# A two-layer graph attention kernel on one core: the order of the encoder's last additions, the place of the decoder's first weights on VectorE, and the queue that stores kept tiles

## Chip, core and metric

The kernel runs on one core of a Trainium2 chip. The metric is the device time of one execution in microseconds (us); the median of several runs counts. Engines are named as in the profile: PE (TensorE), ACT (ScalarE), DVE (VectorE), POOL (GpSimd), SP (SyncE). PEld is PE's loading of weights.

## What is computed

Layer 0, for N = 4096 nodes, 512 features and H = 4 heads of D = 128 (both masks of the layer are the same adjacency matrix, so its two attentions are one):

```python
Xw  = einsum('hnd,hde->hne', Xh, W)              # Xh: relu(layernorm(x)) by heads
sig = sigmoid(f1[:, :, None] + f2[:, None, :])   # f1, f2: Xw times V
att = softmax(where(adj != 0, adj * sig, -inf))  # per head, 4096 x 4096
Xn  = batchnorm(concat_heads(att @ Xw))
emb = batchnorm(elu(Xn @ Wm.T + bm) + Xn)        # encoder's MLP
Y   = elu(concat_heads((att @ Yh) @ W.T))        # Yh: emb by heads; the same att again
out = batchnorm(elu(Y @ Wd.T + bd) + Y)          # decoder's MLP
x   = x + out
```

Layer 1 is a graph attention layer with leaky-relu logits over the same adjacency matrix, with a residual. The change touches layer 0 alone.

## The kernel before

**Blocks and tiles.** `attention` (L221) runs three times: for the encoder (L598), the decoder (L702) and layer 1 (L932). Each run goes over 8 blocks: 4 heads, and for each the two halves `tb` of 2048 target nodes. A block goes over NJ = 32 source groups `j` of 128 nodes. For each `j` a tile `e` of 128 x 2048 fp32 unnormalized weights is made and multiplied on PE with the head's values (L371) into four PSUM banks, one for each 512 targets. In the encoder and decoder the weights come from `tanh_weights` (L448): a tanh on ACT (L450), an exp on ACT (L451) and a multiplication by the mask on DVE (L452).

**Masks.** The adjacency matrix comes as fp32. At the start POOL issues eight DMAs (L481) that cast it to uint8 into DRAM (`masks`). For each tile SP loads 128 x 2048 bytes of it (`load_mask`, L210, 256 KB) into one of five buffers `a`; the load waits until the multiplication five tiles earlier has been done.

**Buffers of weights.** The encoder has eight `e` buffers: two in the pool `keep` (EP = 2), which also the decoder uses, and six of its own. A tile's buffer is used again eight tiles later, when PE, the sums and a store, if there is one, have done with it.

**Denominators.** The sum of the weights over `j` is needed in the encoder. A schedule (ENC and others, L62 to L64) says for each `j` which way is taken: an accumulating DMA of POOL (L386, `moved`), a product with ones on PE (L262, `by_ones`), or else an addition on DVE into `acc` (L394). In the encoder's last block the tiles 30 and 31 go by ones, 26 to 29 by DVE. At the end of a block the sums themselves are multiplied by ones (L405, L407). In the last block the product of tile 31 is left until behind them (`late`, L376 and L423); then come the reciprocal (L435), its spreading on PE (L440), scaling and statistics. The encoder's MLP (`mlp_block`, L605) starts on PE with products of the first three heads (L613).

**Kept tiles.** The decoder needs the same weights again. The encoder (`kept="write"`) stores every fifth tile of a block (j = 4, 9, 14, 19, 24, 29; KEEP = 5) to DRAM in `ekeep`, 1 MB each, 48 in all. The store is issued by ACT three tiles later (L358), the block's last one at tile EVICT = 2 of the next block (through `at`, L292) or, in the last block, at its end (L410). The decoder (`kept="read"`) loads these tiles by SP (L343) instead of making them.

**The decoder's first weights.** Tiles 0 and 1 of the decoder use the two buffers of `keep`, so they can be made before the encoder's pools are released; tile 0 is made in four quarters. `pinned` (L213) makes instructions stand behind given ones in the order of issue.

**The order of the work** on each engine is fixed when the program is built: a scheduler places each instruction on its engine's queue, within the bounds that `issue_after` and `pinned` set; on the chip each queue then runs in that order. DMAs issued by SP, ACT and POOL appear in the profile as the queues q1, q10 and q0.

Of the kernel before, what the change touches and what calls it, by code (L numbers as in the profile page):

```python
# [42 lines left out]
NJ = N // P  # L43
# [27 lines left out]
KEEP = 5  # L71

EP = 2

EVICT = 2
# [10 lines left out]
def kernel(ctx, tc, x, xT, adjT, w0, w0T, v0, wencT, wdecT, vecs, w1, w1T, a1, outT):  # L86
    nc = tc.nc
# [131 lines left out]


    def attention(what, keep, pools, weights, values, row_of, out, finish, ebufs, modes=None, invert=None,  # L221
                  kept=None, sums=None, sums2=None, extras={}, row0=None, masks0=(), in_parts0=1):

# [64 lines left out]
        def at(j, f, *args):  # L290

            later.setdefault(j, []).append(lambda: f(*args))  # L292
# [28 lines left out]
        for n, (h, tb) in enumerate(blocks):  # L321
            last = n == len(blocks) - 1
            moved, by_ones, *ends_later = modes(n) if modes is not None else ((), ())
            den = bank1() if invert is not None else None
            begun = False
            into = sums2[0 if n else 1] if moved else None

            po, ahead, late = [bank() for _ in range(SB - 1)], [], []
            adds, held, stores, next_row = [], [], [], None
            for j in range(NJ):  # L330

                with pinned(products_of):
                    for f in later.pop(j, []):
                        f()
                with pinned([a_load, *products_of, last_main] if j else []):
                    if (n, j) in extras:
                        extras[n, j](a_load)
                    if not last and j == NJ - 10:
                        next_row = next_row_of(*blocks[n + 1])
                e = weight_tile()  # L340
                store = j % KEEP == KEEP - 1 and kept is not None
                if store and kept == "read":
                    a_load = nc.sync.dma_start(e, ekeep[h][tb][j // KEEP])  # L343
                else:
                    if masks0:
                        a, a_load = masks0.pop(0)
                    else:
                        a = mask_tile(keep)
                        a_load = load_mask(a, tb, j)

                    with pinned(products_of[:1] if kept == "read" and n == 0 and j < 8 else []):
                        products_of = weights(e, rowb, a, j, h, SB if NJ * n + j < in_parts0 else 1)
                    if store:
                        stores.append((j // KEEP, e))

                    if j % KEEP == KEEP - 3 and stores:
                        k, t = stores.pop()
                        nc.scalar.dma_start(ekeep[h][tb][k], t)  # L358

                def products():  # L360
                    nonlocal last_main, last_ones

                    with tc.issue_after(last_ones.ins) if last_ones is not None else nullcontext():

                        if j == EVICT:
                            po.append(bank())
                            for k, t in ahead:
                                nc.tensor.matmul(po[-1], block(values[h], k), t[:, (SB - 1) * IB:SB * IB],  # L368
                                                 start=(k == 0), stop=False)
                        for s, b in enumerate(po):  # L370
                            last_main = nc.tensor.matmul(b, block(values[h], j), e[:, s * IB:(s + 1) * IB],  # L371
                                                         start=(j == 0), stop=(j == NJ - 1))
                    last_ones = None


                if last and invert is not None and j >= NJ - (1 if kept is not None else 2):  # L376
                    late.append((j, e))
                else:
                    products()
                if j < EVICT:  # L380
                    ahead.append((j, e))
                if invert is not None:
                    if j in moved:

                        for into_half, e_half in in_parts(2, into, e):
                            nc.gpsimd.dma_start(into_half, e_half, **({"accum_op": ALU.add} if j > moved[0] else {}))  # L386
                    elif j in by_ones:
                        held.append(e)
                    else:
                        adds.append(e)  # L390
                        if len(adds) == 2:
                            nc.vector.tensor_add(acc, *adds)
                        elif len(adds) > 2:
                            nc.vector.tensor_add(acc, acc, e)  # L394

                    if held and j + 1 not in by_ones:
                        with tc.issue_after(last_main.ins):
                            for t in held:
                                add_to_den(den, t, not begun)
                                begun = True  # L400
                        held = []
                    if j == NJ - 1:
                        with tc.issue_after(last_ones.ins) if last_ones is not None else nullcontext():
                            if moved and not ends_later:
                                add_to_den(den, into, not begun)  # L405
                                begun = True
                            add_to_den(den, acc, not begun, not ends_later)  # L407
            for k, t in stores:
                if last:
                    nc.scalar.dma_start(ekeep[h][tb][k], t)  # L410
                else:
                    at(EVICT, nc.scalar.dma_start, ekeep[h][tb][k], t)
            if not last:

                at(EVICT, ending, h, tb, po, den if invert is not None else None,
                   4 if kept == "write" and n == 0 else 0)
                if ends_later:
                    at(1, add_to_den, den, into, False, True)
                rowb = next_row
                continue  # L420
            for s, b in enumerate(po):
                for k, t in late:
                    nc.tensor.matmul(b, block(values[h], k), t[:, s * IB:(s + 1) * IB], start=(k == 0),  # L423
                                     stop=(k == NJ - 1))
            outs = [out(spool, h, tb, s, po[s]) for s in range(SB)]
            if invert is None:
                for s, o in enumerate(outs):
                    rb = spread(h, tb, s)
                    for f in finish:
                        f(spool, h, tb, s, o, rb, True)  # L430
                continue

            inv = spool.tile([P, IB], FP, name="dsb", tag="rb", bufs=3)
            nc.vector.tensor_scalar(inv, den, invert[0], None, invert[1])
            nc.vector.reciprocal(inv, inv)  # L435
            if kept is not None:
                nc.gpsimd.dma_start(rinvs[h][tb].rearrange("o (s i) -> (o s) i", i=IB), inv[0:P:32, :])
            for s, o in enumerate(outs):
                rb = bank()
                nc.tensor.matmul(rb, ident[:, 32 * s:32 * s + 1].to_broadcast([P, P]), inv, start=True, stop=True)  # L440
                for f in finish:
                    f(spool, h, tb, s, o, rb, True)
# [14 lines left out]
    with tc.tile_pool(name="keep", bufs=1) as keep:  # L457
# [147 lines left out]
        def mlp_block(work, w, src, dst, gamma, beta, scale, between, early=None):  # L605
# [11 lines left out]
            for o in range(C):  # L617
# [7 lines left out]
                for ib in range(NIB):  # L625
# [13 lines left out]
                        nc.vector.tensor_add(d, nodes(src[o], ib), ex)  # L639
                    else:  # L640
                        nc.vector.scalar_tensor_tensor(d, nodes(src[o], ib), scale[:, o:o + 1], ex, ALU.mult, ALU.add)
                    nc.vector.bn_stats(stats[:, o, ib, :], d)
                    between(o, ib)
                bn_coefs(stats, gamma, beta, a_mlp, b_mlp, o, o + 1)
            return last_product

        with tc.tile_pool(name="m_small", bufs=1) as small, tc.tile_pool(name="m_work", bufs=3) as work:
# [4 lines left out]
                nc.vector.tensor_add(bias, bias_of(bank1(), C - 1, C)[:, 0:C], bias)  # L652
                scale_weights(C - 1)

            mlp_block(work, w, xc, yc, "enc_mlp_bn_gamma", "enc_mlp_bn_beta", a_att, lambda o, ib: None, last_head)


            for h in range(H):
# [41 lines left out]
        nc.sync.dma_start(w, wdecT.rearrange("(c p) o -> p c o", p=P))  # L700
        with tc.tile_pool(name="dec", bufs=1) as spool:
            attention("dec", keep, spool, tanh_weights, xc, lambda h, tb: (rows[tb], h), out_dec, (scaled, elu), 4,  # L702
                      kept="read", extras={(1, 6): sums_of_weights, (1, 16): bias_of_decoder})


    v1 = xd
# [2 lines left out]
    with tc.tile_pool(name="l_small", bufs=1) as small, tc.tile_pool(name="l_work", bufs=2) as work:  # L709
# [22 lines left out]
                nc.sync.dma_start(outT[o * P:(o + 1) * P, :], x1[o])  # L732
            return added

        def between(o, ib):

            if o in (1, 2):
                residual(o - 1, ib)
            elif o == C - 1 and ib >= NIB // 2:
                residual(o - 1, ib - NIB // 2)  # L740
# [237 lines left out]
```

## Time and profile before

| What | Value |
|---|---|
| Runs shown | 3267.72, 3262.49, 3267.79 us; median 3267.72 |
| Profiled execution | 3260.23 us, of which the span of the core is 3258.4 us |
| PE, DVE, ACT, POOL busy | 98%, 82%, 80%, 15% of the span |
| Encoder's attention | 65 to 1043 us |
| Encoder's MLP | 1055 to 1197 us |
| Decoder's attention | from 1197 us |
| Encoder's ACT in blocks 3 to 6 | 118.7 to 118.8 us each, with 118.6 to 118.7 busy |
| DMA packets | 578.48 MB; q0 36.0%, q1 27.1%, q10 4.8% of 16 engines' span |
| Stores of kept tiles | 48 of 1024 KB, median 7.6 us from issue to landing |
| Loads of masks | 720 of 256 KB, median 4.1 us from issue to landing |

How it is read: times in a timeline are us from the span's start. A group of instructions shows line, engine and operation, then the written tile, an arrow and the read tiles. In brackets stands how long the engine was idle just before, and who ended that. "x2" says that two like instructions were merged. A landing is the end of a DMA, as its semaphore tells it. Busy time of PE is no measure of its peak, since matmuls are pipelined and their ends are modelled; each 128 x 512 fp32 product appears as two records.

### The profile page before, as it was taken

Reading aid. Unit: us, or ns where it says so; the run is one execution under the profiler, and the core shown is the slowest. Engines: PE = TensorE matmul, PEld = TensorE weight load, DVE = VectorE, ACT = ScalarE, POOL = GpSimd, SP = SyncE. Lnnn points to the kernel's source line nnn. Section 1 sums busy time; section 2 is a strip of 40 time slices with the busy share of each in tenths; the row PEclk is TensorE's granted clock in tenths of the full one; section 3 lists DMA queues with packets and bytes.
Section 4 is the critical chain, followed back from the end, with each engine's and each line's share of the span. In section 5 each row is a group of like instructions: output and inputs, shape, how many; then the busy total and the mean of one; then the engine's idle time right before and its main releaser. Section 6 shows DMA issues by size and latency. Waiting matters only on the chain.

```text
span 3258.4 us, 26085 instructions
## 1 busy us (share of the span) xinstructions
PE 3197.5 (98%) x8723; PEld 1484.0 (46%) x8723; DVE 2665.4 (82%) x1933; ACT 2601.8 (80%) x1908; POOL 477.6 (15%) x622
## 2 busy tenths in 40 slices
PE   7999999999999999999999999999999999999999
PEld 6334434444443464444444444448644444444443
DVE  6999999999999675556655565585599999999998
ACT  7999999999997459899999999566765666666664
POOL 2001221211211000000000000025412222122221
PEclk9999999999999999999999999999999999999999
DMA  9997988988986014434443443231488999889995
GB/s 208 196 195 226 259 227 230 266 224 226 268 232 177 4 64 130 147 127 129 153 142 125 139 153 122 78 121 56 129 207 216 218 229 243 214 210 238 218 214 143
DMA packets 211150, 578.48 MB, mean 178 GB/s; under 512 B 25068, under 2 KB 28172, under 8 KB 195016
## 3 DMA queue, kind: packets, MB, share of 16 engines
q0 software_dynamic: 67968, 222.51, 36.0%
q1 hardware_dynamic: 126432, 293.72, 27.1%
q10 hardware_dynamic: 16616, 60.60, 4.8%
q8 instruction: 68, 1.11, 0.1%
q14 instruction: 66, 0.54, 0.0%
HBM read 377.10 MB, written 84.29 MB: 142 GB/s over the span
## 4 chain that ended last, share of the span: by engine, by line
PE 68%; ACT 12%; DVE 9%; issue 7%; DMA 3%; POOL 0%; ACTq 0%; DVEq 0%; POOLq 0%
PE ps L371 52%; ACT e L450 7%; PE ps L613 7%; DVE e L452 5%; ACT e L451 4%; PE ps L809 3%; DMA a<-mask 2%; DVE acc L394 2%; PE den L262 1%; DVE e L904 1%; DVE R L394 1%; PE ps L670 1%; DMA acc<-e 1%; PE ps L368 1%; PE ps L537 1%
## 5 line engine op out<-in xcount | busy, mean ns | idle before, releaser
L371 PE MATMUL ps<-e,R 128*128 128x512 f32 x6024 | 2614.1, 594 | 37.5 <-DVE e L452 35.2
L371 PEld LDWEIGHTS ps<-e,R 128*128 128x128 f32 x6024 | 1140.1, 190 | 1504.8 <-issue 1396.6
L452 DVE TENSOR_TENSOR e<-e,a 128x2048 f32<-128x2048 f32 (+1 forms) x470 | 1051.7, 2259 | 383.7 <-ACT e L451 369.4
L450 ACT ACTIVATE e<-rowb,score 128x2048 f32<-128x2048 f32 (+1 forms) x470 | 912.4, 1968 | 85.9 <-PE ps L371 43.9
L451 ACT ACTIVATE e<-e 128x2048 f32<-128x2048 f32 (+1 forms) x470 | 870.6, 1879 | 6.1
L903 ACT ACTIVATE e<-rowb,nq,jcol 128x2048 f32<-128x2048 f32 x224 | 461.4, 2090 | 273.7 <-DMA w<-e 133.9
L904 DVE SCALAR_TENSOR_TENSOR e<-e,jcol,a 128x2048 f32<-128x2048 f32 (+1 forms) x265 | 591.8, 2267 | 7.3 <-ACT e L903 7.3
L394 DVE TENSOR_TENSOR acc<-acc,e 128x2048 f32<-128x2048 f32 x130 | 297.1, 2286 | 2.1
L394 DVE TENSOR_TENSOR R<-R,e 128x2048 f32<-128x2048 f32 x123 | 280.5, 2281 | 0.0
L386 POOL DMA_DIRECT2D w<-e x178 | 150.3, 847 | 613.4 <-DMA w<-e 356.1
L613 PE MATMUL ps<-R,w 128*128 128x512 f32 x512 | 220.3, 592 | 0.6 <-DVE w L571 0.6
L386 POOL DMA_DIRECT2D acc<-e x144 | 120.4, 881 | 542.9 <-DMA acc<-e 196.8
L287 POOL DMA_DIRECT2D rb<-rinvs x60 | 34.5, 580 | 1059.2 <-DVE R L561 865.9
L613 PEld LDWEIGHTS ps<-R,w 128*128 128x128 f32 x512 | 97.2, 190 | 122.7 <-issue 117.7
L634 ACT ACTIVATE ex<-ps,bias 128x512 f32<-128x512 f32 x64 | 44.0, 687 | 98.8 <-PE ps L613 79.0
L809 PE MATMUL ps<-w1x,hT 128*128 128x260 f32 x512 | 115.5, 384 | 1.4 <-ACT hT L787 1.4
L809 PEld LDWEIGHTS ps<-w1x,hT 128*128 128x128 f32 x512 | 96.5, 190 | 19.9 <-issue 3.3
L903 ACT ACTIVATE e<-w,nq,jcol 128x2048 f32<-128x2048 f32 (+1 forms) x41 | 67.4, 1711 | 24.5 <-DMA R<-e 24.4
L636 DVE SCALAR_TENSOR_TENSOR ex<-ex,re 128x512 f32<-128x512 f32 x64 | 45.0, 702 | 36.4 <-ACT re L635 36.2
L846 POOL TENSOR_TENSOR vacc<-vacc,R 128x128 f32<-128x128 f32 x120 | 65.8, 576 | 45.3 <-ACT R L839 45.0
L839 ACT ACTIVATE R<-ps,rstd 128x128 f32<-128x128 f32 x128 | 38.5, 371 | 29.3 <-PE ps L809 25.6
L262 PE MATMUL den<-e,ones 128*32 128x512 f32 x424 | 51.1, 598 | 0.0
(172 smaller groups left out, 1246.2 us busy)
## 6 DMA issues: line engine op xcount, KB each, us to landing
a<-mask SPq DMA_DIRECT2D x720, 256.0 KB, 4.1
w<-e POOLq DMA_DIRECT2D x178, 512.0 KB, 6.8
acc<-e POOLq DMA_DIRECT2D x144, 512.0 KB, 6.7
ekeep<-e ACTq DMA_DIRECT2D x48, 1024.0 KB, 7.6
e<-ekeep SPq DMA_DIRECT2D x48, 1024.0 KB, 4.9
mask<-in_adjT POOLq DMA_DIRECT2D x8, 2048.0 KB, 99.4
rowb<-rows SPq DMA_DIRECT2D x16, 1024.0 KB, 7.7
rb<-rinvs POOLq DMA_DIRECT2D x60, 256.0 KB, 4.2
```

The costliest lines, as they stand in the source:

```text
L262: last_ones = nc.tensor.matmul(den[s * 32:(s + 1) * 32, :], ones[:, 0:32], t[:, s * IB:(s + 1) * IB], start=start, stop=stop)
L371: last_main = nc.tensor.matmul(b, block(values[h], j), e[:, s * IB:(s + 1) * IB], start=(j == 0), stop=(j == NJ - 1))
L386: nc.gpsimd.dma_start(into_half, e_half, **({"accum_op": ALU.add} if j > moved[0] else {}))
L394: nc.vector.tensor_add(acc, acc, e)
L450: nc.scalar.activation(e, rowb, AF.Tanh, bias=column(score[:, 1], j, h), scale=0.5)
L451: last_act = nc.scalar.activation(e, e, AF.Exp, scale=0.5)
L452: last_dve = nc.vector.tensor_mul(e, e, a)
L613: last = nc.tensor.matmul(z, w[:, fb, o * P:(o + 1) * P], nodes(src[fb], ib), start=(fb == 0), stop=(fb == C - 1))
L809: m = nc.tensor.matmul(banks[k][:, 0:2 * DX], hT[:, fb, c * P:(c + 1) * P], w1x[:, fb, 2 * k:2 * k + 2, :].rearrange("p h x -> p (h x)"), ...
L846: nc.gpsimd.tensor_add(vacc[:, h, :], vacc[:, h, :], block(v1[h], j))
L903: last_act = nc.scalar.activation(e, rowb, AF.Relu, bias=column(nq, j, h), scale=column(jcol, j, h))
L904: last_dve = nc.vector.scalar_tensor_tensor(e, e, column(jcol2, j, h), a, ALU.add, ALU.mult)
```

## The change

It has three parts. In the encoder's last block, additions on DVE of tiles from j = 26 on are collected and issued after the multiplication of tile 31; the first of them may be placed where its operands and the queue allow. The decoder's first two tiles are pinned behind the statistics of the MLP's output block 1, column step 0 (a DVE instruction, L642). The stores of kept tiles are issued by SP instead of ACT, and in the order of the program when the next kept tile is made, five tiles later, instead of three.

```diff
     def attention(what, keep, pools, weights, values, row_of, out, finish, ebufs, modes=None, invert=None,
-                  kept=None, sums=None, sums2=None, extras={}, row0=None, masks0=(), in_parts0=1):
+                  kept=None, sums=None, sums2=None, extras={}, row0=None, masks0=(), in_parts0=1, behind=()):
...
-                    with pinned(products_of[:1] if kept == "read" and n == 0 and j < 8 else []):
+                    with pinned([*(products_of[:1] if kept == "read" and n == 0 and j < 8 else ()),
+                                 *(behind if n == 0 and j < EP else ())]):
                         products_of = weights(e, rowb, a, j, h, SB if NJ * n + j < in_parts0 else 1)
                     if store:
+                        if stores:
+                            k, t = stores.pop()
+                            nc.sync.dma_start(ekeep[h][tb][k], t)
                         stores.append((j // KEEP, e))
-
-                    if j % KEEP == KEEP - 3 and stores:
-                        k, t = stores.pop()
-                        nc.scalar.dma_start(ekeep[h][tb][k], t)
...
                         adds.append(e)
-                        if len(adds) == 2:
+                        if last and kept is not None and j >= NJ - 6:
+                            at_end.append(e)
+                        elif len(adds) == 2:
                             nc.vector.tensor_add(acc, *adds)
                         elif len(adds) > 2:
                             nc.vector.tensor_add(acc, acc, e)
+
+                    if j == NJ - 1:
+                        for t in at_end:
+                            nc.vector.tensor_add(acc, acc, t)
...
             for k, t in stores:
                 if last:
-                    nc.scalar.dma_start(ekeep[h][tb][k], t)
+                    nc.sync.dma_start(ekeep[h][tb][k], t)
                 else:
-                    at(EVICT, nc.scalar.dma_start, ekeep[h][tb][k], t)
+                    at(EVICT, nc.sync.dma_start, ekeep[h][tb][k], t)
...
-                    nc.vector.bn_stats(stats[:, o, ib, :], d)
-                    between(o, ib)
+                    made = nc.vector.bn_stats(stats[:, o, ib, :], d)
+                    between(o, ib, made)
...
+            behind_it = []
+            mlp_block(work, w, xc, yc, "enc_mlp_bn_gamma", "enc_mlp_bn_beta", a_att,
+                      lambda o, ib, made: behind_it.append(made) if (o, ib) == (1, 0) else None, last_head)
...
             attention("dec", keep, spool, tanh_weights, xc, lambda h, tb: (rows[tb], h), out_dec, (scaled, elu), 4,
-                      kept="read", extras={(1, 6): sums_of_weights, (1, 16): bias_of_decoder})
+                      kept="read", behind=behind_it, extras={(1, 6): sums_of_weights, (1, 16): bias_of_decoder})
```

More of the change, by code (lines that the diff above doesn't have):

```diff
@@ L328, in attention @@
             po, ahead, late = [bank() for _ in range(SB - 1)], [], []
-            adds, held, stores, next_row = [], [], [], None
+            adds, held, stores, at_end, next_row = [], [], [], [], None
             for j in range(NJ):
@@ L653, in last_head @@
                 scale_weights(C - 1)
-            mlp_block(work, w, xc, yc, "enc_mlp_bn_gamma", "enc_mlp_bn_beta", a_att, lambda o, ib: None, last_head)
+            behind_it = []
+            mlp_block(work, w, xc, yc, "enc_mlp_bn_gamma", "enc_mlp_bn_beta", a_att,
+                      lambda o, ib, made: behind_it.append(made) if (o, ib) == (1, 0) else None, last_head)
             for h in range(H):
@@ L733, in residual, with between @@
             return added
-        def between(o, ib):
+        def between(o, ib, made):
             if o in (1, 2):
```

## The prediction

> **What bounds the kernel now.** I read the stretches first, then the DMA queues, then the timelines. "Block n, tile j" is head n//2, target half n%2, source group j. Columns of the stretches: us, busy us of PE, PEld, DVE, ACT, POOL with counts, clock, DMA share, GB/s.
>
> ```profile
> 130.00:160.00 30.00, 29.56 (x81) 12.22 (x79) 29.86 (x15) 29.94 (x17) 0.00 (x0) 1.00 1.05 221
> 554.50:673.30 118.80, 116.27 (x305) 49.66 (x304) 114.65 (x65) 118.67 (x66) 22.30 (x29) 1.00 0.88 239
> ```
>
> The second line is encoder block 4: ACT is busy 118.67 of 118.80 us, DVE 114.65, PE 116.27. After 360 us ACT never idles for more than 0.8 us at once, and from 510 us on the chain of waits is mostly ACT L450/L451: the encoder's later blocks are ACT's. The first line lies in block 0: DVE is as full as ACT, and the DMA engines are saturated. There the adjacency is still being cast to the mask (POOL's queue q0, until 237 us):
>
> ```profile
> a<-mask SPq DMA_DIRECT2D x32, 256.0 KB, 13.6
> ekeep<-e ACTq DMA_DIRECT2D x6, 1024.0 KB, 10.1
> ```
>
> That is 80 to 210 us: a mask takes 13.6 us to land, against 4.7 between 600 and 1000 us. Two multiplies wait for one here, the longer:
>
> ```profile
> 167.66 2.29 DVE L452 TENSOR_TENSOR e<-e,a 128x2048 f32<-128x2048 f32 x1 [1.19 <-DMA a<-mask]
> ```
>
> How the rings share the engines shows in packets: without a store (160 to 168 us), with one (134 to 138), and with a 1 MB row load on SP's own ring (150 to 154). Columns: queue, packets, MB, share of 16 engines:
>
> ```profile
> q0 software_dynamic: 330, 0.68, 83.0%
> q1 hardware_dynamic: 330, 0.61, 22.8%
> ```
>
> ```profile
> q0 software_dynamic: 90, 0.18, 45.3%
> q10 hardware_dynamic: 92, 0.75, 44.7%
> q1 hardware_dynamic: 98, 0.17, 12.8%
> ```
>
> ```profile
> q1 hardware_dynamic: 93, 0.68, 41.8%
> q0 software_dynamic: 96, 0.16, 40.5%
> q10 hardware_dynamic: 45, 0.37, 21.9%
> ```
>
> q1 (SP), q10 (ACT) and q0 (POOL) get equal counts. In the last stretch q1 moves the row alone (83 packets of 8 KB and the completions, no mask packet) although three masks had been issued behind it.
>
> ACT in block 4:
>
> ```profile
> 576.67 3.88 ACT L450 ACTIVATE e<-rowb,score 128x2048 f32<-128x2048 f32 x2
> 580.45 1.89 ACT L451 ACTIVATE e<-e 128x2048 f32<-128x2048 f32 x1
> 580.64 0.33 ACTq L358 DMA_DIRECT2D ekeep<-e  x1
> 582.25 1.90 ACT L451 ACTIVATE e<-e 128x2048 f32<-128x2048 f32 x1
> ```
>
> The issue runs beside ACT's work. But near most stores the tanh/exp pairs are broken into single tiles. A pair lasts 7.39 us (547.12 to 554.50), 3.69 a tile; a single tile 3.83 (617.44 to 621.27).
>
> The encoder's end:
>
> ```profile
> 1033.62 4.61 DVE L394 TENSOR_TENSOR acc<-acc,e 128x2048 f32<-128x2048 f32 x2
> 1038.14 6.89 DVE L452 TENSOR_TENSOR e<-e,a 128x2048 f32<-128x2048 f32 x6
> ```
>
> ```profile
> 1031.56 7.13 PE L371 MATMUL ps<-e,R 128*128 128x512 f32 x16 [0.83 <-DVE e L452]
> 1040.48 3.70 PE L371 MATMUL ps<-e,R 128*128 128x512 f32 x8 [1.79 <-DVE e L452]
> 1044.12 1.92 PE L262 MATMUL den<-e,ones 128*32 128x512 f32 x16
> 1045.86 1.90 PE L262 MATMUL den<-acc,ones 128*32 128x512 f32 x16
> ```
>
> ACT has tile 31 ready at 1032.6; its multiply ends at 1042.6, behind two additions. PE waits four times after 1019 (0.63, 0.19, 0.83, 1.79 us).
>
> **The Trainium skill.** "DMA: Bandwidth & Descriptors", section "Queues, rings and completion order": each engine goes round robin over the rows that have work, each row's ring is consumed in order, and SP and ACT own one row each. The trace agrees in both (90:92:98, and the masks behind the row); its grain it does not show. "ScalarE: Activation LUTs", section "What ACT_TABLE_LOAD costs": back-to-back ACTIVATEs overlap by about 93 ns. The trace agrees: a pair gains about 0.1 us at each border, a single tile only at one of its two.
>
> **The change part by part.** Base: the profiled execution, 3260.23 us (span 3258.4), 7.5 below the median of 3267.72; differences are carried over to the median.
>
> *Last additions.* In the built order the multiplies of tiles 26 to 29 go first, one addition, the multiplies of 30 and 31, three additions. DVE has no idle time from 1017 on, so the last addition still ends at 1042.3. Tiles are ready earlier, so PE runs without waits: busy to 1026.84, then tiles 27 to 30 at 3.43 us each to 1040.6, the ones-products of 30 and 31 (1.8) and the moved sum (0.9) to 43.3, the sum of acc 0.9 to 1044.2. Before, this was 1047.7. Tile 31's product, the reciprocal, L440 and L613 follow as before: L613 starts at 1052.1 instead of 1055.5. **-3.4**. It keeps this: from there to 1167 PE has one wait, 0.65. Next late is PE. If the last addition were late by one (2.2), 1.2 would remain.
>
> *Decoder's first multiplies.* Four quarters of 0.60 and one of 2.2 leave 1042 to 1061 us and stand behind the first statistics of output block 1. Only DVE's move; PE's order is identical, ACT's tanh and exp stay. Leaving frees nothing: the coefficients end at 1062.7, PE needs them at 1073.5. Where they go, DVE idles 1.23 us before each of most 512-column steps, so 4.6 us are taken up in four steps; seven PSUM banks cover that; uncovered it would be 4.6. PE wants the tiles at 1196. SP's mask loads 6 and 7 come later, but stood ahead of a load that waits to 1167 anyway. **0**.
>
> *Stores.* 48 issues (0.33 us each) leave ACT and go to SP, each just behind the mask load that waits for the same multiply (five mask buffers), so SP gains no wait but the issue. Behind each stand the next masks, and DVE behind those.
> On ACT: in the built order the tiles run in pairs, so a block is 16 x 7.385 = 118.2 against 118.8. It counts where ACT bounds, block 2 tile 12 to block 7, 5.6 blocks x 0.64 = **-3.6**.
> On the ring, while the cast runs: a mask is 128 packets and 16 completions. Before, a store took 144/23 = 6.3 us, in which 153 of 720 mask packets of five tiles also went; the other 567 at 41 per us take 13.7: 20.0 us per five tiles. DVE's pace, block 0 tile 9 (105.8) to block 1 tile 3 (212.6), is 20.5 including its waits: the ring just keeps up. After, five masks need 17.45 and the store, alternating with the cast, 8 rounds of 0.31 + 0.32, about 5.0: 22.45. So each store holds the masks behind it back by 2.45 us. Six stores come before the cast ends: 14.7. The mask of block 1 tile 3 landed 2.0 us ahead of its multiply, which leaves 12.7; that of tile 0, behind five, 0.1 ahead, which leaves 12.1. The cast gains slots and ends a little sooner, so I take **12** for what DVE loses. Does it reach the end? DVE is full from 205 to 355 us, and ACT's waits in between (277.7 and 360.4, for acc<-e) hang on its multiplies: all of it. Bounds: 0 if I misread the ring, 15 with no slack. The reuse of a stored tile waits for a later landing (10 becomes about 20 us), but ACT leads DVE by up to 13 us there: 0, at worst 3.
> In later blocks masks land 5.6 us or more ahead: 0, bound below.
>
> Sum: 12 - 3.6 - 3.4 = +5.0: 3265.2 for such an execution, **3272.7** for the median.
>
> **Rivals.** *The ring does not starve DVE*, because masks catch up or the cast ends sooner: against it speak the backlog of 15 us and the margin of 0.1; for it, that the cast gains the slots of q10. Then -7.0: 3260.7. *Masks starve later too*: in blocks 2 to 6 acc<-e keeps q0 busy, a store ahead costs about 5 us, and the smallest margin is 5.6. It decides once a mask is late; at 1.0 us for each of six stores, less the 4.1 us that DVE idles per block, 1.9 x 5 = 9.5 more: 3282.2, slower. For it: DMA share 0.88; against: margins are mostly 9 to 15. That the change would not do what it says is excluded by the built order.
>
> **How the numbers follow.** Likeliest 0.48, its own range 3268.7 to 3275.7 (DVE loses 8 to 15); no starving 0.35; later starving 0.17. The range 3259 to 3280 leaves out the upper half of the last and the edge of the second. About 0.2% (6.5 us) can be told from no change. Faster: 0.25 of the second case. Slower: 0.16 of the first and all of the last, 0.33. The same: 0.42.
>
> **What would show it.** Masks of block 0 and 1 landing up to 20 us after issue, DVE waits on a<-mask of about 12 us between 130 and 230; ACT blocks of 118.2; the den products ending 3.4 us sooner after ACT's last exp. No mask waits there would refute the main term.

## The result, and the profile after

| Kernel | Median, us | Runs | Range, us |
|---|---|---|---|
| before | 3266.36 | 22 | 3261.56 to 3273.20 |
| after | 3271.07 | 22 | 3266.46 to 3273.72 |

The ratio is 1.0016, 95% interval 1.0010 to 1.0022: 4.7 us by the medians, 3.3 to 7.2 us by the interval. The forecast was 3272.7 us, +5.0 us on the 3267.72 of the three runs that were shown then.

The two profiled executions lie further apart than the medians, 3273.13 us (span 3271.2) against 3260.23 us (span 3258.4): the one of before is 6.1 us below its median, the one of after 2.1 above. So single spans are not compared below; the same stretches are, in every kernel. The encoder is cut at block starts (ACT's first tanh of a block; in block 0, whose first tile is made in four quarters, the last quarter's), at ACT's last exp of block 7 and at the first product of the MLP (L613, after: L621):

| Stretch, us | before | after | difference |
|---|---|---|---|
| blocks 0 to 2 | 364.8 | 380.4 | +15.6 |
| blocks 3 to 6, each | 118.75 | 118.18 | -0.57 |
| block 7 up to ACT's last exp | 121.8 | 121.2 | -0.6 |
| last exp to the MLP's first product | 22.9 | 19.6 | -3.3 |
| from there to the end | 2202.9 | 2206.3 | +3.4 |

Loss, gains and their places are those of the forecast, apart from the last row. That row is PE's clock. Here is a stretch of the decoder in the kernel after (columns as before: us, busy us and counts of PE, PEld, DVE, ACT, POOL, clock, DMA share, GB/s):

```profile
1340.00:1350.00 10.00, 10.00 (x29) 5.50 (x29) 3.57 (x2) 4.00 (x3) 0.00 (x0) 0.66 0.17 54
```

Over these 10 us PE was granted 0.66 of its clock on the mean, which costs 3.4 us; in the 10 us before it was 1.00. Every kernel below needs 2202.9 to 2206.3 us for this row, and the values do not follow the edits: e1, e7 and e10, which have the change's gains, are at 2203.0 like before, and e4, built like before at the encoder's end, is at 2206.3 like after. So the row belongs to the execution and not to the change.

Now a part of block 0 and block 4, the stretches that answer to the first fence of the prediction:

```profile
130.00:160.00 30.00, 26.52 (x69) 10.80 (x69) 25.84 (x13) 28.80 (x16) 0.00 (x0) 0.95 1.05 189
569.60:687.70 118.10, 117.83 (x309) 50.19 (x307) 114.25 (x64) 118.10 (x65) 22.37 (x29) 1.00 0.89 241
```

In block 0 DVE is busy 25.84 of 30 us where it was 29.86, and the DMA engines move 189 GB/s in place of 221 at the same full share: before, a store took turns in ACT's ring beside the cast and the masks, and now it takes those of the masks. (A ring is the line in which the packets of one queue stand.) In block 4 ACT has no idle time at all and the block is 0.6 us shorter. DMA issues from 80 to 210 us (KB each, median us to landing), then the waits of DVE from 70 to 205 us before and after, and those of ACT after (us in total, times, longest):

```profile
a<-mask SPq DMA_DIRECT2D x29, 256.0 KB, 17.4
ekeep<-e SPq DMA_DIRECT2D x6, 1024.0 KB, 24.9
```

```profile
DVE e L452 <- ACT e L451: 4.9, 4, 2.3
DVE e L452 <- DMA a<-mask: 1.6, 2, 1.2
```

```profile
DVE e L460 <- DMA a<-mask: 14.6, 7, 6.2
DVE e L460 <- ACT e L459: 4.9, 4, 2.3
```

```profile
ACT e L458 <- DMA ekeep<-e: 14.7, 3, 11.2
```

A mask takes 17.4 us to land instead of 13.6, a store 24.9 instead of 10.1. DVE waits 14.6 us for masks, before 1.6. ACT waits as long for stored tiles, before not at all; but DVE's waits for ACT's tiles, 4.9 us in four times, are to the tenth what they were before, and they all lie before 82 us, ahead of the first store at 93.2. The two tiles behind ACT's longest wait (11.2 us, to 178.9) were still ready 4.1 and 6.7 us before their multiplications. So in this kernel it is the masks that end DVE's waits, and not ACT's tiles. That the late tiles would have cost nothing by themselves is not shown: up to there DVE had itself been held up 14 us by masks, so by these numbers the first of the two would otherwise have been some 8 to 10 us late (an estimate). Both delays come from stores in SP's ring, and no run separates them. The chain of waits that ended last holds masks and no stored tile (start us, us, what):

```profile
132.43 2.30 DVE e L460
...
134.74 19.61 DMA a<-mask
...
154.47 2.30 DVE e L460
...
156.79 25.52 DMA a<-mask
...
184.76 20.06 DMA a<-mask
...
207.26 20.12 DMA a<-mask
```

This is a loop: a multiply frees one of five mask buffers, SP issues the next mask into it, that mask stands in the ring behind older masks and a store for 20 to 25 us, and the multiply that ends the wait frees the next buffer. Almost everything from 134 to 227 us on this chain is the ring. It is not SP's own waiting: the new mask is issued at once (the multiplication of 132.43 ends at 134.73, the load starts at 134.74), and so it is, within 0.03 us, for all but one of the mask loads from 95 to 248 us; before, it was the same. What the ring does during one store (172.4 to 177.8 us):

```profile
q0 software_dynamic: 161, 0.30, 54.2%
q1 hardware_dynamic: 163, 1.05, 48.6%
```

One packet of SP for one of the cast, as the prediction read it. The cast's last part lands at 231.2 us instead of 237.5.

The encoder's end on DVE (start us, us):

```profile
1044.20 4.49 DVE L460 TENSOR_TENSOR e<-e,a 128x2048 f32<-128x2048 f32 x2
1048.61 6.94 DVE L402 TENSOR_TENSOR acc<-acc,e 128x2048 f32<-128x2048 f32 x3
...
1057.97 3.35 DVE L443 RECIPROCAL dsb<-dsb 128x512 f32<-128x512 f32 x1
```

The multiplies of tiles 30 and 31 come first, three additions behind them, no decoder multiply before the reciprocal. ACT's last exp ends at 1045.3, the products with ones that give the denominators (`den`) at 1057.2: 11.8 us later, before 15.2.

### The profile page after: what moved, and what is told of

It is laid out like the page before. It is cut to its first block, busy times and chain, and to the rows that moved or that the text cites. A ratio compares the mean times of both kernels' runs of the same rounds, so it can differ in the third digit from the quotient of the medians.

```text
span 3271.2 us, 26153 instructions
## 1 busy us (share of the span) xinstructions
PE 3207.9 (98%) x8723; PEld 1486.5 (45%) x8723; DVE 2662.9 (81%) x1933; ACT 2598.6 (79%) x1908; POOL 478.0 (15%) x622
## 4 chain that ended last, share of the span: by engine, by line
PE 74%; DVE 11%; issue 5%; DMA 5%; ACT 4%; DVEq 0%; ACTq 0%; POOL 0%; POOLq 0%
PE ps L373 58%; PE ps L621 7%; DVE e L460 4%; DVE acc L398 4%; DMA a<-mask 3%; PE ps L820 3%; ACT e L458 2%; PE den L263 2%; DMA acc<-e 1%; ACT e L459 1%; DVE R L398 1%; PE ps L370 1%; PE ps L681 1%; DVE e L915 1%; PE ps L545 1%
## 5 line engine op out<-in xcount | busy, mean ns | idle before, releaser
L914 ACT ACTIVATE e<-rowb,nq,jcol 128x2048 f32<-128x2048 f32 x224 | 461.5, 2090 | 274.0 <-DMA w<-e 121.2
L398 DVE TENSOR_TENSOR acc<-acc,e 128x2048 f32<-128x2048 f32 x126 | 287.8, 2284 | 0.5
L621 PE MATMUL ps<-R,w 128*128 128x512 f32 x512 | 220.3, 592 | 0.7 <-DVE w L579 0.7
L621 PEld LDWEIGHTS ps<-R,w 128*128 128x128 f32 x512 | 97.2, 190 | 122.7 <-issue 117.7
L642 ACT ACTIVATE ex<-ps,bias 128x512 f32<-128x512 f32 x64 | 44.0, 687 | 100.9 <-PE ps L621 81.0
```

Source lines behind the costliest of these rows:

```text
L621: last = nc.tensor.matmul(z, w[:, fb, o * P:(o + 1) * P], nodes(src[fb], ib), start=(fb == 0), stop=(fb == C - 1))
L914: last_act = nc.scalar.activation(e, rowb, AF.Relu, bias=column(nq, j, h), scale=column(jcol, j, h))
```

## The experiments

Theory: a store in SP's ring costs the masks behind it about 2.5 us, only while the cast runs; the later stores gain 0.6 us per block; the encoder's end gains 3.4 through the additions, and the decoder's move is worth nothing. Rivals: the loss is ACT waiting for stored tiles; the loss lies in the later blocks; the decoder's move is not free. Results against before, as a difference of medians and as a ratio over all runs (the two can differ a little):

| Run | Stores on SP | Additions moved | Decoder moved | us | Ratio, 95% interval |
|---|---|---|---|---|---|
| after | all | yes | yes | +4.7 | 1.0016 (1.0010 to 1.0022) |
| e1 | blocks 2 to 7 | yes | yes | -8.5 | 0.9975 (0.9964 to 0.9986) |
| e2 | none | yes | yes | -0.1 | 1.0000 (0.9992 to 1.0008) |
| e3 | all | no | no | +10.4 | 1.0033 (1.0021 to 1.0046) |
| e4 | none | yes | no | +0.3 | 1.0001 (0.9993 to 1.0009) |
| e5 | all | yes | no | +11.9 | 1.0033 (1.0021 to 1.0046) |
| e6 | all | no | yes | +6.2 | 1.0018 (1.0012 to 1.0025) |
| e7 | blocks 2 to 7, others late on ACT | yes | yes | -7.3 | 0.9975 (0.9964 to 0.9985) |
| e8 | all, in halves | yes | yes | +14.6 | 1.0043 (1.0030 to 1.0057) |
| e9 | blocks 1 to 7 | yes | yes | -10.2 | 0.9968 (0.9956 to 0.9980) |
| e10 | every second of 0 and 1, all of 2 to 7 | yes | yes | -4.3 | 0.9987 (0.9981 to 0.9994) |

And the stretches of their profiled executions, in us:

| Kernel | Blocks 0 to 2 | Blocks 3 to 6, each | Last exp to MLP's first product |
|---|---|---|---|
| before | 364.8 | 118.75 | 22.9 |
| after | 380.4 | 118.18 | 19.6 |
| e1 | 366.0 | 118.2 | 19.6 |
| e2 | 366.6 | 118.8 | 22.9 |
| e3 | 379.8 | 118.2 | 27.5 |
| e4 | 369.4 | 118.75 | 22.9 |
| e5 | 377.7 | 118.2 | 27.7 |
| e6 | 379.8 | 118.2 | 20.6 |
| e7 | 367.1 | 118.2 | 19.6 |
| e8 | 388.8 | 118.2 | 19.6 |
| e9 | 365.4 | 118.2 | 19.6 |
| e10 | 370.7 | 118.2 | 19.6 |

Kernels with the same stores differ by up to 4.6 us in the first column, from one execution to the next; the third repeats within 0.2 us.

**e1: the early stores back on ACT.** In the kernel after:

```diff
                         stores.append((j // KEEP, e))
+                    if n < 2 and j % KEEP == KEEP - 3 and stores:
+                        k, t = stores.pop()
+                        nc.scalar.dma_start(ekeep[h][tb][k], t)
...
-                    at(EVICT, nc.sync.dma_start, ekeep[h][tb][k], t)
+                    at(EVICT, (nc.scalar if n < 2 else nc.sync).dma_start, ekeep[h][tb][k], t)
```

> The changed kernel, but the stores of blocks 0 and 1 go back to ACT's queue at their old place; blocks 2 to 7 stay on SP. Theory (a store in SP's ring holds the masks behind it back, only while the cast runs): no DVE wait for a mask of more than 2 us in blocks 0 and 1, block 2 starts within 1 us of before (315.0 us, against 329.9 with the change), blocks 3 to 6 last 118.2 us, and the time is the two gains alone, -7.0 us or more against before (ratio about 0.998). Rival A (the loss comes from later stores competing with POOL's accumulations, or from the decoder's move): no better than the change, +5 us, ratio 1.0016. Rival B (stored tiles come free too late for ACT, anywhere): part of the loss stays, +1 to +3 us.

Measured: -8.5 us; block 2 starts at 314.5 us; blocks 3 to 6 at 118.2; DVE waits 1.8 us for masks up to 205 us. All of the loss is in the stores of blocks 0 and 1, and the later blocks keep their gain. Rival A falls. Rival B falls for blocks 2 to 7; in blocks 0 and 1 the edit takes away late masks and late stored tiles together.

**e2: all stores on ACT as before, the other two parts kept.** The edit restores the lines of before around the stores.

> The changed kernel with all its stores back on ACT's queue at their old places: the last additions and the decoder's move alone. Theory: encoder blocks as before (block 2 starts at 315 us, blocks 3 to 6 last 118.8 us), the den products end 3.4 us sooner after ACT's last exp (11.7 instead of 15.1 us), and the time is -3.4 us, ratio 0.9990. Rival (the decoder's move is not free): up to 4.6 us back, +1.2 us, ratio 1.0004.

Measured: no change, and 22.9 us at the encoder's end, as before to the tenth. My theory is wrong here, and so is the rival's reason: nothing was gained that the decoder's move could give back.

**e3: the stores alone.** The kernel before with only the store lines of the change.

> The kernel before with only its stores moved to SP's queue. Theory: block 2 starts about 12 to 15 us late, blocks 3 to 6 last 118.2 us, the den products end 15.1 us after ACT's last exp as before, and the time is +8.4 us to +10 us, ratio 1.0026 to 1.0031, the slowest of the four. Rival (the loss lies in the other two parts): not slower than before, -3.6 us, ratio 0.9989.

Measured: +10.4 us, just above what was expected, and by another sum: blocks 0 to 2 lose 15.0, and the encoder's end takes 27.5 us instead of 22.9. DVE there:

```profile
1052.34 6.90 DVE L451 TENSOR_TENSOR e<-e,a 128x2048 f32<-128x2048 f32 x6
1059.16 1.90 DVE L556 COPY R<-ps 128x512 f32<-128x512 f32 x3
...
1062.55 3.35 DVE L434 RECIPROCAL dsb<-dsb 128x512 f32<-128x512 f32 x1
```

The den products even end sooner, 12.9 us after the last exp (which ends at 1044.7) instead of 15.2, but five multiplies of the decoder (four are quarters) and four copies now stand ahead of the reciprocal, which starts at 17.9. So moving the stores cost 4.6 us at that end too.

**e4: the additions alone.** The kernel before with `at_end` and its loop.

> The kernel before with only the last additions behind all multiplies; the decoder's first multiplies stay where they were, and the stores too. Theory: -3.4 us, ratio 0.9990, the same as with the decoder's move, which I hold to be worth 0. Rival (the decoder's move carries the gain of the encoder's end by clearing DVE): about 0 us, ratio 1.0000.

Measured: no change. DVE's order at the end, in the kernel of this run:

```profile
1039.80 4.61 DVE L400 TENSOR_TENSOR acc<-acc,e 128x2048 f32<-128x2048 f32 x2
1044.33 6.89 DVE L458 TENSOR_TENSOR e<-e,a 128x2048 f32<-128x2048 f32 x6
...
1054.74 3.35 DVE L441 RECIPROCAL dsb<-dsb 128x512 f32<-128x512 f32 x1
```

Two additions stand ahead of the last multiplies, instruction for instruction the order of the kernel before. The edit issues the additions late in the program, but the scheduler places them where it did before. In e2 they stand there too, only the decoder's multiplies behind them are gone. As long as the stores are on ACT, this part of the change does nothing.

**e5 and e6: one of the two parts left out, with the stores on SP.** e5 drops `behind=behind_it` from the decoder's call; e6 is the kernel after with

```diff
-                        if last and kept is not None and j >= NJ - 6:
+                        if False:
                             at_end.append(e)
```

> The changed kernel without the decoder's move: the decoder's first multiplies stand where they stood before. In the built order the four quarter multiplies (0.60 us each) then go between and behind the last additions, and one of 2.2 us and the four copies go ahead of the reciprocal. My step called the decoder's move worth 0. With the stores gone from ACT the built order says otherwise: the reciprocal ends about 5.4 us later, of which the four copies (2.4 us), no longer behind it, come back. Theory now: MLP's first product 3 us later after ACT's last exp than with the change (22.6 against 19.6 us), +3 us on the changed kernel, about +8 us against before, ratio 1.0025. Rival (as predicted, 0): the same as the changed kernel, ratio 1.0016.

> The changed kernel without the moved additions: the last additions go alternately with the last multiplies, the decoder's move and the stores on SP stay. Theory: tile 31's multiply ends 10.0 us after ACT's last exp instead of 3.4, the MLP's first product 22.9 us after it instead of 19.6: +3.3 us on the changed kernel, about +8.3 us against before, ratio 1.0026. Rival (the additions carry nothing, the decoder's move carries all of the gain at the encoder's end): the same as the changed kernel, ratio 1.0016.

Measured: the end takes 27.7 us in e5 and 20.6 in e6, against 19.6. So the move of the decoder's multiplies is worth 8.1 us in this order, more than I had worked out, and the additions 1.0 instead of 3.3. e6 cannot be told from the kernel after by its time. DVE and PE in e5:

```profile
1052.47 1.28 DVE L460 TENSOR_TENSOR e<-e,a 128x512 f32<-128x512 f32 x2
...
1055.09 2.28 DVE L460 TENSOR_TENSOR e<-e,a 128x2048 f32<-128x2048 f32 x1
1057.29 1.88 DVE L565 COPY R<-ps 128x512 f32<-128x512 f32 x3
1059.09 3.35 DVE L443 RECIPROCAL dsb<-dsb 128x512 f32<-128x512 f32 x1
```

```profile
1062.49 6.77 PE L448 MATMUL ps<-dsb,ident 128*128 128x512 f32 x8 [5.30 <-DVE dsb L443]
```

```profile
1062.00:1066.00 4.00, 3.51 (x4) 1.51 (x5) 1.80 (x3) 0.00 (x0) 0.57 (x1) 0.50 0.02 6
```

Quarters, a full multiply of the decoder and copies stand ahead of the reciprocal, which ends 21.05 us after the last exp instead of 16.0: 5.1 us, near the 5.4 that I had worked out. Two things I had wrong. The copies that now come early win nothing back, since PE goes from the spreading (L448) straight to the MLP and doesn't wait for them. And PE idles 5.30 us for the reciprocal (0.57 in the kernel after), and its clock is then 0.50: the eight records of the spreading take 6.77 us instead of 3.70, 3.1 us more. The Trainium skill has this: "TensorE: Matmul & The Clock Gate", section "Part 1: The HAM clock gate (the "warmup" mystery)", says that PE's clock is gated down to half after a window of about 3.4 us without work. The trace agrees: after 0.57 us of idle time the clock stays at 1.00, after 5.30 us here and 4.77 us in e3 it is 0.50. How long a wait is needed, these two don't show.

**e7: early stores on ACT at the new, later place.**

```diff
-                            nc.sync.dma_start(ekeep[h][tb][k], t)
+                            (nc.scalar if n < 2 else nc.sync).dma_start(ekeep[h][tb][k], t)
...
-                    at(EVICT, nc.sync.dma_start, ekeep[h][tb][k], t)
+                    at(EVICT, (nc.scalar if n < 2 else nc.sync).dma_start, ekeep[h][tb][k], t)
```

> The changed kernel with the stores of blocks 0 and 1 on ACT's queue, but left at the new place, two tiles later than before: the masks' ring is free of them, and the stored tiles come back to ACT about as late as in the changed kernel. Theory (masks behind stores cost the time, late tiles do not, since ACT leads DVE): ACT waits 10 to 25 us in all for stored tiles in blocks 0 and 1, DVE waits under 3 us for masks, block 2 starts at 315 to 318 us, and the time is -5 to -8 us against before, ratio 0.9975 to 0.9985. Rival (the late reuse of the stored tiles cost the time): block 2 starts near 330 us, +5 us, ratio 1.0016.

Measured: -7.3 us; DVE waits 1.6 us for masks up to 205, and block 2 starts at 309.9 us, sooner than the 315 to 318 expected. But ACT did not wait for stored tiles at all, since on its own ring they land early enough. So the run shows that the ring counts and not the later place; the test of the late tiles that it was meant to be, it is not.

**e8: each store in two halves.**

```diff
-                            nc.sync.dma_start(ekeep[h][tb][k], t)
+                            for half in (slice(0, TB // 2), slice(TB // 2, TB)):
+                                nc.sync.dma_start(ekeep[h][tb][k][:, half], t[:, half])
```

The store at EVICT is cut in the same way.

> The changed kernel with each store cut into two halves by columns: the same bytes in 256 packets of 4 KB in place of 128 of 8 KB. Theory (the ring gets one packet for each packet of the cast, so a store costs the masks behind it packets times the cast's 0.32 us plus its own time): a store takes 16 rounds of 0.16 + 0.32 = 7.7 us of the ring while the cast runs instead of 5.0; six stores cost about 16 us more: block 2 starts near 345 us (330 with the change) and the time is about +20 us against before, ratio 1.006. Rival (bytes decide, not packets): as the changed kernel, block 2 at 330 us, ratio 1.0016.

Measured: +14.6 us, about 10 more than the kernel after. Packets from 180 to 188.8 us, in which one such store passes:

```profile
q0 software_dynamic: 313, 0.64, 71.6%
q1 hardware_dynamic: 315, 1.10, 33.4%
```

From its first packet to its last the same megabyte now takes 8.0 to 9.1 us while the cast runs instead of 5.1 to 6.1, since it comes in twice as many packets and each still waits for one of the cast. Bytes do not decide. Block 0 takes 144.8 us instead of 130.6: +14.2, near the 16 expected. Blocks 1 and 2 give back 5.8 of this (244.0 instead of 249.8 us), which I had not counted: the cast ends at 228.0 us, when block 1 is 13 us old in place of 30 in the kernel after, and from then on masks land early again.

**e9 and e10: how many stores, and which.** e9 is e1 with `n < 1` in both places; in e10 the condition of e1 is `n < 2 and j // KEEP % 2 and ...`, and the store at EVICT stays on SP.

> The changed kernel with the stores of block 0 alone on ACT's queue at their old place; those of block 1 and later stay on SP. Theory (only stores issued while the cast runs cost, and of block 1's at most the first is): blocks 0 and 1 together last 244 to 247 us (244.1 before, 258.9 with the change), time -6 to -8 us against before, ratio 0.9975 to 0.9982. Rival (stores in SP's ring hurt in block 1 as well, cast or no cast): half of the 14.8 us stays, about 251 us, ratio about 0.9995.

> The changed kernel with every second store of blocks 0 and 1 on ACT's queue at its old place, so that three instead of six go through SP's ring while the cast runs. Theory (each store costs its share of the ring, less one slack of about 2.6 us): six cost 14.8 + 2.6 = 17.4 or 2.9 each, three cost 8.7 - 2.6 = 6 us: blocks 0 and 1 together 250 us, time about 9 us better than the changed kernel, ratio about 0.999. Rival (once the ring starves the whole is lost, or the late stored tiles are what counts): 256 to 259 us, ratio 1.001 to 1.0016.

Measured: e9 -10.2 us, with blocks 0 and 1 together 240.2 us and blocks 0 to 2 365.4; e10 -4.3 us, with 247.5 and 370.7. e9 is the fastest kernel of the study, though its interval overlaps those of e1 and e7. It is faster than the -6 to -8 us expected, and its blocks 0 and 1 are shorter than the 244 to 247; at the end of block 2 it is level with before (364.8), so that the surplus is not explained. DVE's waits in e10 from 70 to 205 us:

```profile
DVE e L464 <- DMA a<-mask: 8.9, 4, 6.5
DVE e L464 <- ACT e L463: 4.9, 4, 2.3
```

ACT waits 7.0 us for a stored tile in the same stretch, and again DVE's waits for ACT stay at 4.9 us. By the column of blocks 0 to 2, with e1, e7 and e9 (mean 366.2) as no store in the ring: three stores cost 4.5 us, six 13.2 (mean of after, e3, e5, e6: 379.4). The loss grows with the number of stores in the ring. Whether the first of them cost less is not certain: three stores cost a third of six by this column, in which equal kernels differ by up to 4.6 us, but DVE's waits for masks from 70 to 330 us are 1.6 us before, 8.9 in e10 and 19.0 in the kernel after, which is nearly in proportion.

## Why the prediction was right, and where its reasons were not

- **Stores while the cast runs, +12: right, mechanism and size, as far as the stores in SP's ring go.** The mean of blocks 0 to 2 is 366.9 us with the stores on ACT (before, e2, e4) and 379.4 with them on SP: +12.5. The single pair of profiles says +15.6. The slope from three to six stores is (13.2 - 4.5) / 3 = 2.9 us a store, forecast 2.45. A store took 5.1 to 6.1 us of the ring, forecast 5.0. The sign that was named came larger than forecast: from 130 to 230 us DVE waits 19.0 us for masks, not about 12. e8 shows that packets are what is counted, e9 that only stores issued during the cast matter.
- **Pairs on ACT, -3.6: right.** 0.57 us in each of blocks 3 to 7 make -2.9; the rest of what I had counted lies in block 2, in the row above.
- **Later masks, 0: right.** From 330 to 1040 us DVE never waits for a mask.
- **Reuse of stored tiles, 0: nothing of it shows at DVE, but the reason is open.** I expected that ACT's lead hides it; ACT waits 14.7 us in block 0. DVE does not feel it here (its unchanged 4.9 us, the 4.1 us of lead left), but DVE was late through the masks as well. No run took the late tiles alone, so how the 12.5 us would divide between the two is not shown.
- **Last additions, -3.4: the sum is right (-3.3), its owner is wrong.** My step read the order of the whole changed kernel, so its sum is no luck, but it gave all of the gain to the additions. Alone they are worth nothing (e2, e4), with everything else in place 1.0 (e6).
- **Decoder's first multiplies, 0: wrong.** "Leaving frees nothing" holds in the order of before, where they stand in DVE's wait for the den products. Once the stores have left ACT, the scheduler puts them and the copies ahead of the reciprocal: +4.6 (e3), and +8.1 against the whole change (e5), about 3 us of it PE's half clock. The decoder's move keeps them out. Added in this order, the three parts at the encoder's end are +4.6 for the stores, -6.9 for the decoder's move (27.5 to 20.6), -1.0 for the additions: -3.3. In another order the shares differ: on the stores alone the additions change 27.5 to 27.7 (e5). Where the multiplies went, they cost nothing, as forecast: in the kernel after PE is busy 35.00 of 35.00 us from 1085 to 1120, and they lie at 1104.7 to 1117.2.
- **Total:** 12.5 - 2.9 - 3.3 = +6.3 us, forecast +5.0, measured +4.7 by medians, 3.3 to 7.2 by the interval. That forecast and medians lie within 0.3 us owes something to luck, since equal kernels differ by more than that in the first stretch.

The first rival, no starving, is what e1, e7 and e9 give (-7.3 to -10.2 us; forecast -7.0): it is the kernel without the early stores on SP. The second, masks starving in later blocks, does not happen.

Why the order changes with the stores is left open. What the trace shows is that before, ACT's last store waits for a multiply until 1.2 us after the last exp and ACT's first decoder tanh follows at +1.9 us; with the stores on SP that tanh starts at -0.1. Decoder tiles that are ready 2 us sooner may have been placed sooner for that, but the scheduler's own estimates are in no profile.

## What to carry to other kernels

A queue is a line, not only an issuer: before a large transfer is moved to another engine's queue, count what stands behind it there, in packets against those of the busiest other queue, in each phase of the kernel; here the same move gained 0.6 us in each of five blocks and lost 2 to 3 us for each store issued while the cast ran, and moving only the late ones kept the gain. When a scheduler fixes the order, parts of a change do not add up: read the order that each part alone would build, not only that of the whole. And price a wait of PE not by its length alone: in e5 5.3 us of waiting cost 3.1 us more in clock.

## What the runs showed of the hardware that was not expected

- After 4.77 and 5.30 us without work PE's clock was 0.50, and records of 0.59 us took 1.06 for the next 6 us: about 3 us lost beyond the wait. In all twelve traces the clock's records are 1.00 or 0.50 and nothing between, and each full stretch at 0.50 lasts 3.41 or 6.83 us, as here; a value like 0.66 is the mean over the stretch asked for.
- PE's clock also fell to 0.50 in the decoder where PE's record shows no idle time, in the kernel after from 1341.2 to 1348.0 us, while 32 products of a single column (L705, 4.05 us from 1338.18) ended. Every kernel here has these products. Near their end the clock fell for 6.83 us in after, e3, e4 and e5, for 3.41 us in e2, e6, e8 and e9, and not at all in before, e1, e7 and e10, which cost 3.4, 1.7 and 0 us: the stretch from the MLP's first product to the end takes 2206.3, 2204.6 and 2203.0 us accordingly. Why one execution has it and another not is open; for this alone single executions differ by up to 3.4 us.
- From 130 to 160 us the DMA engines were fully busy before and after the change, yet moved 221 and 189 GB/s: a full share says nothing of bytes. A packet of the cast took 0.32 us for 2 KB written, as long as one of 8 KB of a store; one of a mask, also 2 KB, took 0.10.
